# Layer 1 attention: when the value products of heads 0 to 3 are issued

## The chip, the cores and the metric

The kernel runs on one core of a Trainium2 chip, as one launch. The metric is the device time of that core in microseconds (us). A core has five engines that each run their own instruction stream in order: TensorE (PE, with its weight loads shown apart as PEld), VectorE (DVE), ScalarE (ACT), GpSimd (POOL) and SyncE (SP), which in this kernel issues most of the DMAs. Engines wait for each other by semaphores. Matrix products land in PSUM[...].

## The reference

Two residual attention blocks over x of 8 samples, 512 channels, 32x32 pixels (1024 tokens), all in float32, 8 heads of 64 channels. Layer 0 is ordinary attention. Layer 1, which the change concerns, mixes the heads' scores before the softmax and normalises the weights of each head over the whole map after it:

```
x = x + layer0(groupnorm(x))
x = x + layer1(groupnorm(x))

# layer1, per sample
q, k, v = w_q @ xf, w_k @ xf, w_v @ xf          # (8 heads, 64, 1024)
attn = einsum('bhdq,bhdT->bhqT', q, k) * scale  # scores
attn = einsum('gh,bhqT->bgqT', w_head, attn)    # mixed over heads
attn = softmax(attn, axis=-1)
attn = (attn - mean) / sqrt(var + EPS)          # mean, var of each head's whole map
attn = attn * in_gamma + in_beta
out  = einsum('bhqT,bhdT->bhqd', attn, v)       # value products
out  = out @ w_proj.T + b_proj
```

## The kernel before

Layer 0 takes the first 1813 us; then layer 1 goes through the 8 samples one after the other. All matrix products are float32. A sample has 4 blocks of 256 queries (QB) and 4 blocks of 256 keys (KB), and the work is cut into half steps, `half_step(x, ag)` (L1879), with x from 0 to 36. Each half step does parts of three stages, at three places in the same pipeline:

- Scores of half step x, `scores(x, i)` (L1645), for i = 0 and 1: 8 products of 64x64 weights with 256 columns into one PSUM tile. The tile is copied to the buffer `raw`, by VectorE (L1671) for i = 0 in odd half steps and by ScalarE (L1673) otherwise. Through DMAs of 256 KB, `regroup` (L1675, issue L1682), `raw` is rearranged to `re`, heads onto partitions. There are 32 half steps with scores.
- The mix over heads of half step y = x - 4 (MLAG, L1283), `mix(y, j)` (L1695), for j = 0 and 1: 32 products of 64x64 weights with 64 columns (L1706) into one PSUM tile, then an exponential on ScalarE (L1712) from there into `e`. The epool has two such tiles (L1269).
- For half step w = x - 5: the sums of e and e squared (`squares` on ScalarE, L1723; `sum_e` and `sum_e2` on VectorE, L1730 and L1734), and the value products `values(w, 0)` for heads 0 to 3 and `values(w, 1)` for heads 4 to 7 (L1740): 4 products each of 128x64 weights with 256 columns (L1752), which accumulate over 8 half steps in two PSUM tiles `acc[0]` and `acc[1]`, one buffer each (L1274).

In float32 each product shows as two matmuls and two weight loads in the profile, so a group of scores is 16 matmuls, a mix 64, a group of values 8. Scores and mixes share a rotation of three PSUM tiles (`ps_m`, L1275): a group may start when the group three tiles earlier has been copied out. Value products have tiles of their own.

The order on every engine is the order in which the code calls things. On TensorE a half step is scores 0, mix 0, values 0, scores 1, mix 1, values 1. After the last mix or values instruction a regroup DMA is triggered, one for each call, and after scores a `piece` (L1687): a part of the next sample's input or weights. Eight regroup DMAs make one `re` tile, over two half steps.

Every 8th half step (`first`, L1881: x = 13, 21 and 29) the accumulators of the query block just finished have to be copied out by `leave` (L1762; heads 0 to 3 by ScalarE, L1774, heads 4 to 7 by VectorE, L1772) before new value products may start in them. At the end of the half step before it stands `totals` (L1776), the column sums. Half steps 0 to 3 have scores alone, half step 4 scores and mix, and from x = 32 (NX) on there are no more scores: the last five half steps are mix and value products, with projection products of the next sample between them, put there by an agenda (`ag`), which also runs normalisations, reciprocals and divisions at given half steps.

Of the kernel before, what the change touches and what calls it, by code (L numbers as in the profile page):

```python
# [467 lines left out]
def tile_two_attention_layers(  # L468
# [796 lines left out]
    with ExitStack() as l1:  # L1265
# [14 lines left out]
        NX = 2 * NQB * NKB  # L1280
# [181 lines left out]
        def k_leave():  # L1462
            for fn in due:
                fn()
            due.clear()
# [173 lines left out]
        class Attention1:  # L1639
# [239 lines left out]
            def half_step(self, x, ag):  # L1879
                y, w = x - MLAG, x - MLAG - 1  # L1880
                first = 0 < w < NX and w % QLAG == 0  # L1881
                if first:

                    self.scores(x, 0)
                    self.leave(w // QLAG - 1)
                if 0 <= w < NX:
                    self.squares(w, 0)
                    self.sum_e(w, 0)
                if x < NX and not first:
                    self.scores(x, 0)  # L1890
                if 0 <= w < NX:
                    self.squares(w, 1)
                    self.sum_e(w, 1)
                k_leave()
                if 0 <= w < NX:
                    self.sum_e2(w, 0)
                    self.sum_e2(w, 1)
                if 0 <= y < NX:
                    self.mix(y, 0)
                if 0 <= w < NX:  # L1900
                    self.values(w, 0)
                if x < NX:
                    self.scores(x, 1)
                if 0 <= y < NX:
                    self.mix(y, 1)
                ag.run(x - 0.75)
                if x <= MLAG or x >= NX:
                    self.regroup(n=NR)
                if x >= NX:
                    self.piece(n=len(self.pieces))  # L1910
                ag.run(x - 0.5)
                if 0 <= w < NX:
                    self.values(w, 1)
                    self.e.pop(w)
                    if w % QLAG == QLAG - 1:
                        qb = w // QLAG
                        self.totals(qb)
                        if qb < NQB - 1:
                            ag.at(x + 2, lambda: self.reciprocals(qb, ag, x + 2))
                            ag.at(x + 6, lambda: self.divide(qb))  # L1920
                ag.run(x)
# [139 lines left out]
```

## Time and profile before

| what | us |
|---|---|
| median of 3 runs (4268.31 to 4270.03) | 4268.98 |
| the profiled execution | 4269.45 |
| its span in the profile | 4267.5 |
| first scores of layer 1, sample 0, start at | 1813.3 |
| layer 1, from one sample's first scores to the next's | 309 to 323 |
| mean granted TensorE clock, share of full speed | 0.997 |

Section 5 of the page gives the groups of instructions with their busy time, the mean length of one and the idle time ahead of them. Those of layer 1's half steps:

```profile
L1706 PE MATMUL m<-wmix,re 64*64 64x64 f32 x32768 | 591.0, 219 | 22.4 <-issue 19.7
L1712 ACT ACTIVATE e<-m 128x1024 f32<-128x1024 f32 x512 | 528.1, 1032 | 147.1 <-PE m L1706 142.6
L1752 PE MATMUL a<-e,v 128*64 128x256 f32 x4096 | 556.3, 392 | 25.0 <-ACT q L1774 20.9
L1656 PE MATMUL s<-k,q 64*64 64x256 f32 x8192 | 555.8, 389 | 5.8 <-DVE q L1512 2.6
L1673 ACT COPY raw<-s 128x1024 f32<-128x1024 f32 x368 | 373.4, 1015 | 251.9 <-PE s L1656 229.6
L1671 DVE COPY raw<-s 128x1024 f32<-128x1024 f32 x144 | 176.0, 1223 | 102.5 <-PE s L1656 93.8
```

To read a line: the source line, the engine, the operation, what it writes and reads, the tile of the array (64*64 is 64 rows by 64 columns of it[...]), the shape, the count; then busy us and the mean in ns; then the engine's idle time just ahead and what ended most of it. "issue" means that the trace shows nothing that the engine waited for. The mean of a matmul is longer than its share of the busy time, because several run at once.

In the timeline, a line is a merged run of like instructions of one engine: start and length in us, engine, line, operation, what it writes and reads, count, and idle time ahead in brackets.

### The profile page before, as it was taken

The page shows a single profiled execution, that of the slowest core. Times are in us where ns is not written, and L with a number is a line of the kernel's source. Part 1 is how long each engine was busy: PE and PEld are TensorE (multiplying, and loading weights), DVE is VectorE, ACT ScalarE, POOL GpSimd, SP SyncE. Part 2 cuts the span into 40 slices and gives each one's busy share as a digit, 9 for nine tenths or more (in the row PEclk, how much of TensorE's full clock was granted, in tenths as well). Part 3 has the DMA queues.
Part 4 walks back from the last instruction along what each step waited for, and adds up shares of the span by engine and source line. Part 5 has one row for each costly group of instructions (what it writes and reads, how often), then busy time and mean ns, then how long its engine had stood idle before and what let it go on. Part 6 is the DMA issues. An engine that isn't in the chain of part 4 may idle for free.

```text
span 4267.5 us, 131379 instructions
## 1 busy us (share of the span) xinstructions
PE 4158.3 (97%) x58572; PEld 2213.3 (52%) x58572; DVE 2862.8 (67%) x3780; ACT 2319.2 (54%) x2735; POOL 53.3 (1%) x86
## 2 busy tenths in 40 slices
PE   7999999999999999999999999999999999999998
PEld 4353535353535353466466466466466466465565
DVE  4748484848484848558668668578578578587587
ACT  1717171727272726268268278187187286286385
POOL 0000000000000000000000000000000000000000
PEclk9999999999999999999999999999999999999999
DMA  4213131212121212167377287277386385485474
GB/s 148 78 49 109 47 110 45 86 45 85 45 85 45 84 47 83 56 169 192 111 180 190 93 199 186 99 197 185 96 202 166 103 205 155 121 204 142 136 179 136
DMA packets 253872, 521.99 MB, mean 122 GB/s; under 512 B 51889, under 2 KB 59441, under 8 KB 246641
## 3 DMA queue, kind: packets, MB, share of 16 engines
q1 hardware_dynamic: 248416, 510.71, 42.4%
q8 instruction: 461, 7.55, 0.7%
q0 software_dynamic: 2576, 0.69, 0.3%
q10 hardware_dynamic: 2304, 2.10, 0.2%
q14 instruction: 115, 0.93, 0.1%
HBM read 197.16 MB, written 46.92 MB: 57 GB/s over the span
## 4 chain that ended last, share of the span: by engine, by line
PE 90%; DVE 4%; ACT 2%; DMA 2%; issue 1%; SPq 0%; POOL 0%; DVEq 0%; ACTq 0%; POOLq 0%
PE a L1752 11%; PE s L1656 11%; PE m L1706 11%; PE s L1083 10%; PE a L1109 10%; PE pp_p L903 5%; PE pk_p L903 5%; PE pq_p L903 4%; PE pv_p L903 4%; PE pk L1400 4%; PE pq L1400 4%; PE pv L1475 4%; PE pp L1400 3%; PE t L1783 2%; ACT q L1774 1%
## 5 line engine op out<-in xcount | busy, mean ns | idle before, releaser
L1706 PEld LDWEIGHTS m<-wmix,re 64*64 64x64 f32 x32768 | 580.8, 135 | 117.1 <-issue 57.5
L1088 ACT ACTIVATE e<-s 128x1024 f32<-128x1024 f32 x512 | 497.2, 1026 | 234.2 <-PE s L1083 233.8
L1706 PE MATMUL m<-wmix,re 64*64 64x64 f32 x32768 | 591.0, 219 | 22.4 <-issue 19.7
L1712 ACT ACTIVATE e<-m 128x1024 f32<-128x1024 f32 x512 | 528.1, 1032 | 147.1 <-PE m L1706 142.6
L1752 PE MATMUL a<-e,v 128*64 128x256 f32 x4096 | 556.3, 392 | 25.0 <-ACT q L1774 20.9
L1730 DVE TENSOR_TENSOR z<-z,e 128x1024 f32<-128x1024 f32 x448 | 537.8, 1218 | 62.3 <-ACT e L1712 62.3
L1734 DVE TENSOR_TENSOR z<-z,e 128x1024 f32<-128x1024 f32 x448 | 534.2, 1219 | 44.4 <-ACT e L1723 43.7
L1656 PE MATMUL s<-k,q 64*64 64x256 f32 x8192 | 555.8, 389 | 5.8 <-DVE q L1512 2.6
L1096 DVE TENSOR_TENSOR zacc<-zacc,e 128x1024 f32<-128x1024 f32 x384 | 468.6, 1220 | 90.4 <-ACT e L1088 69.3
L1673 ACT COPY raw<-s 128x1024 f32<-128x1024 f32 x368 | 373.4, 1015 | 251.9 <-PE s L1656 229.6
L1083 PE MATMUL s<-q,k 64*64 64x512 f32 x4096 | 490.1, 593 | 2.3 <-ACT e L1088 2.3
L1109 PE MATMUL a<-e,v 64*64 64x512 f32 x4096 | 484.1, 589 | 0.0
L1723 ACT ACTIVATE e<-e 128x1024 f32<-128x1024 f32 x448 | 461.7, 1062 | 0.0
L1656 PEld LDWEIGHTS s<-k,q 64*64 64x64 f32 x8192 | 267.7, 132 | 272.9 <-issue 169.4
L1752 PEld LDWEIGHTS a<-e,v 128*64 128x64 f32 x4096 | 250.8, 136 | 147.1 <-ACT q L1774 24.2
L1109 PEld LDWEIGHTS a<-e,v 64*64 64x64 f32 x4096 | 156.7, 133 | 282.8 <-issue 282.8
L1083 PEld LDWEIGHTS s<-q,k 64*64 64x64 f32 x4096 | 147.9, 133 | 275.2 <-issue 241.4
L1671 DVE COPY raw<-s 128x1024 f32<-128x1024 f32 x144 | 176.0, 1223 | 102.5 <-PE s L1656 93.8
L1475 PE MATMUL pv<-re,y 128*128 128x512 f32 x480 | 214.5, 600 | 0.0
L1475 PEld LDWEIGHTS pv<-re,y 128*128 128x128 f32 x480 | 89.1, 191 | 113.3 <-issue 112.6
L903 PE MATMUL pv_p<-left_v,tmp 128*128 128x256 f32 x512 | 115.0, 383 | 4.2 <-DVE tmp L932 4.2
L1480 DVE COPY v<-pv 128x512 f32<-128x512 f32 x30 | 20.7, 689 | 139.6 <-ACT v L1479 139.6
(315 smaller groups left out, 4050.3 us busy)
## 6 DMA issues: line engine op xcount, KB each, us to landing
re<-raw SPq DMA_DIRECT2D x1024, 256.0 KB
rzb<-zd SPq DMA_DIRECT2D x256, 128.0 KB
left_q<-left_q SPq DMA_DIRECT2D x17, 1792.0 KB
left_p<-left_p SPq DMA_DIRECT2D x17, 1792.0 KB
left_k<-left_k SPq DMA_DIRECT2D x10, 1792.0 KB
x<-in_x_dram SPq DMA_DIRECT2D x32, 512.0 KB
x<-x SPq DMA_DIRECT2D x64, 256.0 KB
left_v<-left_v SPq DMA_DIRECT2D x8, 1792.0 KB
```

The source lines that it names most:

```text
L903: nc.tensor.matmul(out, st, mv, start=start, stop=(k == 1), skip_group_check=True)
L1083: nc.tensor.matmul(ps[c * D : c * D + D, m], k[r, hp, k0 : k0 + D], q[r, hp, ts(f, FB)], start=True, stop=True,)
L1088: nc.scalar.activation(e[i], ps, AF.Exp, scale=S0 * S0)
L1109: nc.tensor.matmul(acc[g][a][m * D : m * D + D], v[rows, kc, ts(2 * hp + m, D)], e[i][rows, m], start=(kc == 0), stop=(kc == NG - 1),)
L1400: nc.tensor.matmul(self.ps[m][:, i], w[:, left, k * HC + i * P : k * HC + i * P + P], right[:, k], start=(k == 0 and m != 2), stop=(k == 1 ...
L1475: nc.tensor.matmul(ps[:, m], y_t[b][:, c, ts(2 * i + m, P)], w[:, c], start=(c == 0), stop=(c == NCC - 1),)
L1656: last = nc.tensor.matmul(pv[c * D : c * D + D, m, j], qo_t[b][r, 2 * qb + j, hp, ts(c, D)], k_t[b][r, hp, ts(kb, KB)], start=True, stop=True,
L1706: last = nc.tensor.matmul(ps[c * D : c * D + D, a, ts(r, D)], self.re[t, r][rows, j, k0 : k0 + D], wmix[rows].rearrange("p g i -> p (g i)" ...
L1712: nc.scalar.activation(self.e[y][:, j], ps.rearrange("p a c -> p (a c)"), AF.Exp)
L1730: nc.vector.tensor_add(self.z[:, j], self.z[:, j], self.e[y][:, j])
L1734: nc.vector.tensor_add(self.z2[:, j], self.z2[:, j], self.e2[j])
L1752: last = nc.tensor.matmul(self.acc[w][two * D : two * D + D, s].rearrange("p (c i) -> p c i", i=Q8), v_t[b][:, kc, ts(g, D)], e[:, g], sta ...
```

## The change

The call of `values(w, 0)` is moved from behind the first mix of the half step to its end, ahead of `values(w, 1)`, and behind the agenda's slots x - 0.75 and x - 0.5.

```diff
@@ half_step @@
                 if 0 <= y < NX:
                     self.mix(y, 0)
-                if 0 <= w < NX:
-                    self.values(w, 0)
                 if x < NX:
                     self.scores(x, 1)
                 if 0 <= y < NX:
                     self.mix(y, 1)
                 ag.run(x - 0.75)
...
                 ag.run(x - 0.5)
                 if 0 <= w < NX:
+                    self.values(w, 0)
                     self.values(w, 1)
                     self.e.pop(w)
```

On TensorE a half step becomes scores 0, mix 0, scores 1, mix 1, values 0, values 1. The regroup DMA that `values(w, 0)` triggers moves with it on SP's queue: it now follows the one of the second mix. No instruction is added or taken away, and no buffer changes.

## The prediction

> **What bounds the kernel now.** I read the page first, then the busy time of two full half steps, then TensorE's timeline through an ordinary half step, through the odd places and through a stall. The page:
>
> ```profile
> PE 4158.3 (97%) x58572; PEld 2213.3 (52%) x58572; DVE 2862.8 (67%) x3780; ACT 2319.2 (54%) x2735; POOL 53.3 (1%) x86
> q8 instruction: 461, 7.55, 0.7%
> PE 90%; DVE 4%; ACT 2%; DMA 2%; issue 1%; SPq 0%; POOL 0%; DVEq 0%; ACTq 0%; POOLq 0%
> ```
>
> TensorE is busy 97% of the span and is 90% of the chain of waits. Remember the second line: 58572 matmuls and 58572 weight loads come in 461 instruction blocks of 16 KB. The view by windows (two half steps; PE, PEld, DVE, ACT, POOL, clock, DMA share, GB/s) and the timeline of one half step (start, length):
>
> ```profile
> 2485.00:2497.00 12.00, 12.00 (x364) 8.55 (x359) 10.42 (x10) 10.78 (x12) 0.00 (x0) 1.00 0.86 222
> ```
>
> ```profile
> 2307.85 1.09 PE L1656 MATMUL s<-k,q 64*64 64x256 f32 x16
> 2308.77 1.11 PE L1706 MATMUL m<-wmix,re 64*64 64x64 f32 x64
> 2309.81 1.08 PE L1752 MATMUL a<-e,v 128*64 128x256 f32 x8
> 2310.82 1.09 PE L1656 MATMUL s<-k,q 64*64 64x256 f32 x16
> ```
>
> TensorE never rests, ScalarE and VectorE are at 87 to 90%. From start to start, scores to mix take 0.91 us, mix to value products 1.04, value products to scores 1.01: 2.97 us, twice per half step, 5.94. [...] Two places show other neighbours:
>
> ```profile
> 2783.54 1.11 PE L1706 MATMUL m<-wmix,re 64*64 64x64 f32 x64
> 2784.47 1.05 PE L1656 MATMUL s<-k,q 64*64 64x256 f32 x16
> 2785.34 0.97 PE L1706 MATMUL m<-wmix,re 64*64 64x64 f32 x51
> 2787.65 0.45 PE L1706 MATMUL m<-wmix,re 64*64 64x64 f32 x13 [1.34 <-issue]
> ...
> 2379.48 1.95 PE L1752 MATMUL a<-e,v 128*64 128x256 f32 x16
> ```
>
> Mix to scores is 0.93, the scores to mix after it 0.87, and two groups of value products end to end take 1.95, so the second costs 1.95 - 1.08 = 0.87. The fourth line shows something else: TensorE stands for 1.34 us in the middle of a group, released by nothing the trace shows ("issue"). Counting matmuls and their loads from 2783.54, 128 + 32 + about 96 = 256 instructions have been issued: one 16 KB block. The DMA view, cut into narrow windows, puts one instruction packet at 2785.22, lasting 0.96 us. TensorE goes on 1.47 us after its end. [...] Two stalls a block apart in an ordinary half step say the same, 4.02 us:
>
> ```profile
> 3720.21 1.09 PE L1706 MATMUL m<-wmix,re 64*64 64x64 f32 x58 [0.47 <-issue]
> 3721.22 1.08 PE L1752 MATMUL a<-e,v 128*64 128x256 f32 x8
> 3722.24 1.09 PE L1656 MATMUL s<-k,q 64*64 64x256 f32 x16
> 3723.15 0.87 PE L1706 MATMUL m<-wmix,re 64*64 64x64 f32 x46
> 3724.23 0.50 PE L1706 MATMUL m<-wmix,re 64*64 64x64 f32 x18 [0.20 <-issue]
> ```
>
> Last, the steps marked `first` in the code, where the accumulators must be copied out:
>
> ```profile
> 2321.51 1.08 PE L1752 MATMUL a<-e,v 128*64 128x256 f32 x8 [0.87 <-ACT q L1774]
> ...
> 2327.27 1.01 ACT L1673 COPY raw<-s 128x1024 f32<-128x1024 f32 x1
> ```
>
> The first value products stand 0.94 us longer than 1.04 (24 times, 22.6 us). Over all mix-to-value steps of layer 1 the timeline has 64.8 us above 1.04 each; the other 42 us are almost all block stalls.
>
> [...] 64x64 to 128x64 and back costs 1.04 and 1.01, staying in a mode 0.87 to 0.93. [...]
>
> **The change, part by part.** It adds and removes nothing; each half step's order on TensorE goes from s m a s m a to s m s m a a.
>
> *Transitions.* After: 0.91 + 0.93 + 0.87 + 1.04 + 0.87 + 1.01 = 5.63 or 5.64 us against 5.94: 0.30 less. Per sample, half steps 5 to 31 have all three parts, 27; six belong to the `first` pairs below. The other 21 x 8 x 0.30 = 50.4 us. In half steps 32 to 35 (mix and values, then projection work) m a m a becomes m m a a; no row shows m after m, but same-mode steps are 0.87 to 0.93, so about 0.3 again: 4 x 7 x 0.3 = 8.4. Two mixes in a row use up a block in 1.9 us, which costs stalls (below), so I take 5.4; the bounds are 0 and 8.4. The last sample has no projection there and VectorE sums take four times 1.14, 4.6 us, a step: nothing.
>
> *Score tiles.* Scores and mixes rotate through three PSUM tiles, so the second mix needs the first scores copied out. It comes 2.71 us after the first scores start, formerly 3.97. Copy on VectorE (odd half steps): 1.09 + 0.07 + 1.22 = 2.38; on ScalarE 2.17. Both fit, by 0.26 and 0.5 us with the semaphore's 0.07, if the engine is free. ScalarE's six operations in an even half step start 0.92 apart, 5.5 us; VectorE's nine in two half steps 1.14 apart, 10.3 of 11.3 us. Both keep up. Behind the waiting mix stand only the value products. One sample's normalisation plus division before half step 27 makes VectorE late by about 0.44, with crumbs elsewhere: 3.5 us in all.
>
> *`first` steps.* Value products now come after the second mix, 3.75 us in, and ScalarE has left the accumulators at 2.85: the 0.94 goes. But ScalarE is back to back from there: its next first-score copy (2327.27 above) ends 9.67 us after the step's start whatever TensorE does, and the second mix needs it at 5.63 + 2.71 = 8.34. It waits 1.40. The pair takes 9.74 + 1.04 + 0.87 + 1.01 = 12.66 against 12.91: 24 x 0.25 = 6.0 us.
>
> *Instruction blocks.* Weight loads and matmuls are 32, 128 and 16 per s, m and a: 352 a half step, 11 blocks in 8. Formerly the shortest block, from a mix's start, was 1.04 + 1.01 + 0.91 + 0.66 = 3.62 us; now m s m have no values between them and it is 0.93 + 0.87 + 0.78 = 2.58. Of the eleven positions, those under 4.0 us were 3.62 three times and about 3.7; now 2.59, 2.99 and 3.18, others 4.27 up. With 4.0 us a block, 8 half steps lost 3 x 0.38 + 0.3 = 1.44, 27 such sets 39 us, which the 42 confirm; now 1.41 + 1.01 + 0.82 = 3.24, 88 us. So 49 us more. Where ScalarE's 1.40 falls with a stall they overlap, some 0.4 us in each of 24 pairs: 10 back.
>
> *DMA and SP.* Regroup DMAs are triggered by the ends of mixes and values, one each, so three now follow each other (1.0 us apart), then two pieces and one regroup. All eight per tile still precede the next tile's scores, the last one behind a mix instead of values, so their landing has 4.5 us instead of 3.8 until its use. SP's order follows TensorE's; nothing is queued longer. Cost nothing, except that the DMA share, 0.86 there, rises by a twentieth, which can lengthen the block fetch.
>
> Sum: 50.4 + 5.4 + 6.0 - 3.5 = 58.3 us without the blocks, - 49 + 10 = 19.3 with them. The profiled execution took 4269.45 (span 4267.5 and 1.95 around it), so 4250; the median of the runs, 4268.98, is 0.5 less, within the rounding.
>
> **Rivals.** *The fetch does not grow.* [...] the 2.58 us blocks then cost no more than now: 4269.45 - 58 = 4211. Against it: the first half step with mixes (s m s m) shows that stall in seven of eight samples. *The score-tile wait takes the gain.* If VectorE or ScalarE starts the first copy 0.3 us later than laid out, on top of the margins, each half step gives back its 0.30, the blocks then get their old time, and some 4267 is left, no change. For it: both engines are near 90%; against it: stalls give them time. *Slower, by the block fetch.* Place: the second mix of a half step. If three regroups in a row and the denser DMA lengthen a block from 4.0 to 4.3 us, the stalls become 118, 79 more than now: 4269.45 - 58 - 10 + 79 = 4280; at 4.5 us 152, so 4314. It decides from 4.2 us on. For it: with the DMA engines 80 to 95% busy the packet starts 1.5 us after the block before it is begun (median), with under 30%, 0.8 us.
>
> **How the numbers follow.** Forecast 4250 (own range 4228 to 4261) 0.5; fetch unchanged 0.12; score tiles 0.17; slower 0.21. The range 4210 to 4284 leaves out the far ends of the first and last. A change within 0.2%, 8.5 us, is not told from none: faster 0.59 (most of the forecast and the second case), same 0.20, slower 0.21.
>
> **What would show it.** Right: value products as groups of 16 matmuls of 1.95 us; ordinary half steps without a stall at 5.63; no wait for the accumulator copies; the second mix of the half step after a `first` one waiting for ScalarE's copy of scores; "issue" idle time in mixes about doubled, by 0.8 to 1.4 us each. Wrong: half steps all alike above 5.7 with a wait for a score copy, which would mean that the tiles bind; or "issue" time unchanged.

## The result, and the profile after

The changed kernel takes 4306.05 us (median of 4 runs, 4303.42 to 4309.25), the kernel before beside it 4269.5: the ratio is 1.0084, 95% interval 1.0071 to 1.0097. It is 0.84% slower, where I had forecast a gain of 0.45%. It is one of the rivals that came true: the wait for instruction blocks.

From the page of the changed kernel, the busy times and the groups that were shown of before (busy, mean ns | idle before, and what ended it):

```profile
PE 4115.0 (96%) x58572; PEld 2222.7 (52%) x58572; DVE 2862.6 (67%) x3780; ACT 2303.1 (54%) x2735; POOL 53.4 (1%) x86
...
q8 instruction: 461, 7.55, 0.7%
...
PE 84%; ACT 5%; DVE 4%; issue 4%; DMA 3%; SPq 0%; ACTq 0%; DVEq 0%
```

```profile
L1706 PE MATMUL m<-wmix,re 64*64 64x64 f32 x32768 | 599.7, 220 | 102.2 <-issue 82.2
...
L1656 PE MATMUL s<-k,q 64*64 64x256 f32 x8192 | 551.0, 384 | 14.3 <-ACT e L1712 5.8
L1752 PE MATMUL a<-e,v 128*64 128x256 f32 x4096 | 512.9, 390 | 14.8 <-issue 14.5
```

TensorE does the same instructions in 43 us less busy time (4115.0 against 4158.3; the value products alone 512.9 against 556.3), and the span is 36 us longer. The idle time ahead of mixes went from 22.4 to 102.2 us, 82.2 of it "issue". In the chain, TensorE fell from 90% to 84% and issue rose from 1% to 4%.

The timeline of TensorE in the changed kernel, a half step without a stall and the start of the next:

```profile
2503.81 1.09 PE L1656 MATMUL s<-k,q 64*64 64x256 f32 x16
2504.73 1.11 PE L1706 MATMUL m<-wmix,re 64*64 64x64 f32 x64
2505.66 1.05 PE L1656 MATMUL s<-k,q 64*64 64x256 f32 x16
2506.52 1.11 PE L1706 MATMUL m<-wmix,re 64*64 64x64 f32 x64
2507.57 1.95 PE L1752 MATMUL a<-e,v 128*64 128x256 f32 x16
2509.44 1.09 PE L1656 MATMUL s<-k,q 64*64 64x256 f32 x16
```

The steps are close to those forecast: scores to mix 0.92, mix to scores 0.93, scores to mix 0.86, the value products in one group of 1.95. The half step takes 5.63 us. But in many others TensorE stands in the middle of a group, for nothing that the trace shows. From one of these places to the next in a sample it is a multiple of 128 matmuls, that is of 256 instructions with the weight loads, to within one or two matmuls. The page has 461 packets of 16 KB on the instruction queue for 2 x 58572 matmuls and loads, 254 to a packet. So I read these places as the ends of instruction blocks.

Such a stall, with what SP issued ahead of it:

```profile
2891.19 1.11 PE L1706 MATMUL m<-wmix,re 64*64 64x64 f32 x64
2892.12 1.05 PE L1656 MATMUL s<-k,q 64*64 64x256 f32 x16
2892.99 0.87 PE L1706 MATMUL m<-wmix,re 64*64 64x64 f32 x47
2896.16 0.50 PE L1706 MATMUL m<-wmix,re 64*64 64x64 f32 x17 [2.30 <-issue]
2896.59 3.61 PE L1752 MATMUL a<-e,v 128*64 128x256 f32 x16
```

```profile
2888.53 2.39 SPq L1682 DMA_DIRECT2D re<-raw  x3
2891.43 0.48 SPq L1321 DMA_DIRECT2D left_k<-left_k  x1
2892.36 0.53 SPq L1682 DMA_DIRECT2D re<-raw  x1
2893.22 0.48 SPq L1321 DMA_DIRECT2D left_k<-left_k  x1
```

And the DMA view of the 5 us from 2891 to 2896 (queue, packets, MB, share of the 16 engines):

```profile
q1 hardware_dynamic: 638, 1.12, 97.6%
q8 instruction: 1, 0.02, 1.6%
```

The block began near 2891.2, the start of the first mix. Just before, three regroups of 256 KB had been issued in 2.4 us, and the DMA engines are 99% busy in the view (97.6 and 1.6). Narrow windows put the one instruction packet at 2893.42, lasting 1.24 us, and TensorE goes on 1.50 us after its end. So this block took 5.0 us, where the prediction had reckoned 4.0.

The same reading over all half steps 5 to 31: from the start of a block to the start of the next block's packet, plus the packet's length, plus the 1.48 us that passed in the median from its end to the next instruction where TensorE stood. Call this the fetch time. For the blocks that begin within 0.4 us of the start of a first mix its median is 3.61 us before (52 blocks) and 4.09 after (55 blocks), the upper quartile 4.01 and 4.82. Idle time at block ends ("block stalls"), over all of layer 1, is 36 us before and 120 us after (every stretch over 0.36 us, less 0.1 of ordinary spacing).

The last line of the stall shows one thing more: the value products take 3.61 us instead of 1.95. The view by windows (PE, PEld, DVE, ACT, POOL, granted clock, DMA share, GB/s) has the granted clock at 0.50 there:

```profile
2897.00:2900.00 3.00, 3.00 (x16) 1.43 (x12) 2.54 (x3) 1.66 (x2) 0.00 (x0) 0.50 0.47 110
```

Half steps 5 to 30 of the changed kernel have five such stretches of 3.4 us, each behind a stall of 1.9 to 2.3 us; together they cost 7.7 us. The kernel before has none there. Six other stalls in these half steps, of 1.95 to 2.42 us, and one of 2.62 us ending at 2983.68 have none behind them; what decides isn't settled. The mean granted clock was 0.993 to 0.996 in the four runs of the changed kernel, 0.997 in the kernel before.

Where the 36 us come from, by the starts of the groups:

| part of the trace | before | after | difference |
|---|---|---|---|
| half steps 5 to 30, 8 samples, at the pace without stalls | 1302.4 | 1248.0 | -54.4 |
| the same, time above that pace | 39.0 | 136.9 | +97.9 |
| from half step 31 to the end of a sample's value products | 383.1 | 373.8 | -9.3 |
| the rest of the span | | | +2.1 |

Of the 97.9 us in the second row, block stalls in these half steps are 79 (27.5 before, 106.5 after); 19 are other losses, the 7.7 us at half clock among them.

### The profile page after: what moved, and what is told of

The parts are those of the page before. It is cut to its first block, busy times and chain, and to the rows that moved or that the text cites. A ratio compares the mean times of both kernels' runs of the same rounds, so it can differ in the third digit from the quotient of the medians.

```text
span 4303.8 us, 131247 instructions
## 1 busy us (share of the span) xinstructions
PE 4115.0 (96%) x58572; PEld 2222.7 (52%) x58572; DVE 2862.6 (67%) x3780; ACT 2303.1 (54%) x2735; POOL 53.4 (1%) x86
## 4 chain that ended last, share of the span: by engine, by line
PE 84%; ACT 5%; DVE 4%; issue 4%; DMA 3%; SPq 0%; ACTq 0%; DVEq 0%
PE s L1083 10%; PE m L1706 10%; PE a L1109 10%; PE a L1752 10%; PE s L1656 8%; PE pp_p L903 5%; PE pk_p L903 4%; PE pq_p L903 4%; PE pv_p L903 4%; PE pk L1400 4%; PE pq L1400 4%; PE pv L1475 4%; PE pp L1400 3%; PE t L1783 2%; DMA re<-raw 2%
## 5 line engine op out<-in xcount | busy, mean ns | idle before, releaser
L1706 PE MATMUL m<-wmix,re 64*64 64x64 f32 x32768 | 599.7, 220 | 102.2 <-issue 82.2
L1752 PE MATMUL a<-e,v 128*64 128x256 f32 x4096 | 512.9, 390 | 14.8 <-issue 14.5
L1752 PEld LDWEIGHTS a<-e,v 128*64 128x64 f32 x4096 | 276.6, 138 | 166.3 <-issue 43.3
```

What stands on the lines that cost most here:

```text
L1706: last = nc.tensor.matmul(ps[c * D : c * D + D, a, ts(r, D)], self.re[t, r][rows, j, k0 : k0 + D], wmix[rows].rearrange("p g i -> p (g i)" ...
L1752: last = nc.tensor.matmul(self.acc[w][two * D : two * D + D, s].rearrange("p (c i) -> p c i", i=Q8), v_t[b][:, kc, ts(g, D)], e[:, g], sta ...
```

## The experiments

Theory F: the loss is the wait for instruction blocks, which are used up faster in the new order and also arrive later, since three regroup DMAs in a row crowd the DMA engines. Theory G: the arrival is no later by the crowding. Theory S: the time is lost in waits for the PSUM tiles of scores. All times are beside the kernel before on the same chip, which took about 4277 us there; so ratios are compared. The code excerpts leave lines out.

**Regroups in pairs, last one later.** The new order on TensorE stays; the second mix's trigger goes to the second scores.

```diff
 # scores(x, i)
                 if x > MLAG:
                     self.piece(last)
+                if x > MLAG and i == 1:
+                    self.regroup(last)
 # mix(y, j)
-                self.regroup(last)
+                if j == 0 or y + MLAG >= NX:
+                    self.regroup(last)
```

> The changed order on TensorE (s m s m a a), but the regroup DMA that the second mix of a half step triggers is triggered by the second scores instead, so that regroups come in pairs (gaps of about 1, 2, 1, 2 us) as in the kernel before, not three in a row. Theory F (an instruction block takes 4.5 instead of 4.0 us because three regroups in a row crowd the DMA engines): block stalls fall from about 137 us in half steps 5 to 31 to near 88, time about 4257. Theory G (the round trip stays as long as in the changed kernel whatever the bunching; only the amount of DMA traffic and the short blocks count): 4300 to 4310. Theory S (score-tile waits cost the time): no change, 4300 to 4310.

Measured: 4286.05, ratio 1.0024 (1.0017 to 1.0031). Over two thirds of the loss are gone, more than G or S allow, but not all that F expected. The waits of its TensorE (total, times, longest) say what came in their place:

```profile
PE m L1708 <- issue: 52.1, 57, 2.1
PE m L1708 <- DMA re<-raw: 23.1, 34, 1.8
PE m L1708 <- ACT raw L1675: 12.1, 19, 0.7
```

Block stalls are 80 us, and the fetch time of blocks beginning at a first mix is 3.72 us in the median, near the 3.61 before the change. But the last regroup of a tile now stood behind the second scores, nearer to its use, and mixes wait for regrouped scores, which cost 1.7 us in the changed kernel.

**Regroups in pairs, last one as in the changed kernel.** The trigger of the second value products goes to the first scores of the next half step.

```diff
 # scores(x, i)
+                if x > MLAG and i == 0:
+                    self.regroup(last)
 # values(y, w)
-                self.regroup(last)
+                if w == 0:
+                    self.regroup(last)
```

> The changed order (s m s m a a); the regroup DMA that the second group of value products triggers is triggered by the first scores of the next half step instead. So regroups come in pairs as in the kernel before, and the last of each tile is still behind a mix, 4.5 us ahead of its use, while the run with spread regroups had it 3.6 us ahead and waited for it. Theory F (three regroups in a row lengthen the block fetch): stalls for blocks near 80 us as in the spread run, without its waits for regrouped scores: about 4255 to 4265 beside 4269 of the kernel before. Theory G (crowding does not matter; the spread run only moved time about): 4290 to 4310.

Measured: 4280.23, ratio 1.0004 (0.9996 to 1.0011). One DMA trigger of four, moved by one group, takes back 0.8 of 0.84%. Its waits:

```profile
PE m L1708 <- issue: 60.5, 71, 2.1
PE m L1708 <- ACT raw L1675: 15.8, 23, 0.7
PE m L1708 <- DMA re<-raw: 7.5, 12, 1.8
```

Block stalls are 91 us by the count used above, near the 88 of the prediction; the fetch time of blocks that begin at a first mix is 3.59 us. G falls. The expected 4255 to 4265 (beside 4269) is missed all the same: with pairs the new order is no faster than the old, only as fast.

**Three in a row in the old order.** The converse: s m a s m a with the first mix's trigger at the first scores.

```diff
 # scores(x, i)
+                if x > MLAG and i == 0:
+                    self.regroup(last)
 # mix(y, j)
-                self.regroup(last)
+                if j == 1:
+                    self.regroup(last)
```

> The order of the kernel before (s m a s m a), but the regroup DMA that the first mix triggers is triggered by the first scores of the half step instead, so that three regroups follow each other 1 us apart as in the changed kernel. Theory F: the block takes about 4.5 us here too, and the stalls rise from 39 towards 110 us: 4310 to 4340. Theory G: the traffic is the same, so about 4269, at most 4280. Theory S: 4269.

Measured: 4279.61, ratio 1.0009 (1.0000 to 1.0018). F's numbers are wrong here: some 4 us, not 40 to 70; by the time alone G fits as well. Block stalls rise from 36 to 41 us. In half steps 5 to 19 the run is not quite the converse that was meant: the first scores trigger a piece of 128 KB ahead of the regroup, so that SP's queue has one between the second regroup and the third.

```profile
2497.57 1.52 SPq L1684 DMA_DIRECT2D re<-raw  x2
2499.61 0.31 SPq L1356 DMA_DIRECT2D y<-x  x1
2499.97 0.53 SPq L1684 DMA_DIRECT2D re<-raw  x1
```

The closest three regroups of a half step are issued within 2.44 us there (median, first to third), not within 1.86 as in the changed kernel, and the fetch time at a first mix is 3.85 us, against 3.73 before and 4.34 in the changed kernel. In half steps 20 to 30 few pieces are left, and this is the closer comparison (22 to 24 blocks in each median):

| half steps 20 to 30 | three regroups within, us | fetch time at a first mix, us | block stalls, us |
|---|---|---|---|
| kernel before | 2.86 | 3.51 | 8 |
| this run | 2.06 | 3.99 | 10 |
| changed kernel | 1.86 | 4.05 | 38 |
| pairs, last one later | 2.77 | 3.71 | 26 |
| pairs, last one as in the changed kernel | 2.73 | 3.45 | 26 |

Here the fetch gets nearly as long as in the changed kernel, against G, and the old order still loses only 2 us more. So here crowding cost little where the shortest block lasts 3.62 us (10 us of block stalls against 8), and more together with the short blocks of the new order (38 us against 26 with pairs).

**A quarter of the regroup traffic, both orders.**

```diff
 # regroup, from the third key block of each sample on
-    dma = nc.sync.dma_start(out=self.re[t, r], in_=self.raw[t][r::NR])
+    rows = P // NR if t < 2 else P // NR // 4
+    dma = nc.sync.dma_start(
+        out=self.re[t, r][: rows * H], in_=self.raw[t][r::NR][:rows]
+    )
```

> The changed kernel with a quarter of each regroup DMA (from the third key block of each sample on, 4 of the 16 rows are moved, the rest of the regrouped scores stays as it was), so the mix reads partly old scores. Theories F and G (the time is lost waiting for instruction blocks): with the DMA engines mostly idle a block takes about 0.8 + 0.95 + 1.47 = 3.2 us, only the blocks of 2.6 and 3.0 us still stall, some 20 us: 4306 - 137 + 20, about 4190, and some 40 us faster than the light version of the kernel before. Theory S: the waits for score copies stay, so it is not faster than the light version of the kernel before.

> The kernel before with a quarter of each regroup DMA (as in the light version of the changed kernel). Theories F and G: no block under 3.6 us is left to stall, 4269 - 39 = 4230. Theory S says nothing of it beyond 4230 to 4269.

Both kernels leave out three quarters of each of these regroups and serve for their times alone. Measured: 4194.1 in the new order, ratio to the full kernel before 0.9806 (0.9790 to 0.9822), and 4234.0 in the old order, 0.9899 (0.9883 to 0.9916). TensorE's waits in layer 1, first the new order, then the old:

```profile
PE m L1709 <- ACT raw L1673: 17.8, 24, 0.7
PE m L1709 <- issue: 15.5, 27, 1.3
```

```profile
PE a L1755 <- ACT q L1777: 20.9, 24, 0.9
PE m L1709 <- issue: 5.1, 5, 1.4
```

This settles between F and S. With the DMA engines 29% busy (0.86 in the full kernel before, in the same 12 us), the change makes the kernel 40 us faster, as expected: 58 of the sum without blocks, less some 20 for blocks too short even then. The waits for score copies are all still there in the new order (17.8 us, 16.4 in the changed kernel) and aren't what costs. The light runs also take part of the traffic away from every other transfer, so not all of their gain is the block fetch. In half steps 5 to 30 the time above the pace falls by 107 us in the new order, 87 of them block stalls, and by 32 in the old, 19 of them block stalls; the issue time in mixes falls from 82.2 to 15.5 and from 19.7 to 5.1.

**An order with space around each mix.** Scores, scores, mix, values, values, mix: the same single change of tile (64*64 to 128*64) and back, but at least 3.2 us to a block, as I estimated from the steps of the trace. The excerpt is shown against the changed kernel.

```diff
 # half_step
+                if x < NX:
+                    self.scores(x, 1)
                 ...
                 if 0 <= y < NX:
                     self.mix(y, 0)
-                if x < NX:
-                    self.scores(x, 1)
+                if 0 <= w < NX:
+                    self.values(w, 0)
+                    self.values(w, 1)
                 if 0 <= y < NX:
                     self.mix(y, 1)
```

> Another order of the half step: both scores, first mix, all value products, second mix (s s m a a m). It has one change of tiling mode and back, like the changed kernel, but 1.9 us of other work on either side of each mix, so that the shortest instruction block is 3.2 us instead of 2.6. Regroups: first scores, second scores, first mix, second mix in odd half steps; first scores, first mix, first values, second mix in even ones, the last of a tile behind a first mix. Theory F: half steps of 5.62 us, and with 4.0 to 4.2 us a block stalls of 30 to 65 us (216 half steps): 4230 to 4260, below the kernel before. If the time of the changed kernel came from waits for PSUM tiles or accumulators (theory S), this one, with more distance between a group and the reuse of its tile, would also fall to 4230 or lower, but then with its block stalls unchanged at 120 us or more it would not: 4290.

Measured: 4300.66, ratio 1.0056 (1.0042 to 1.0070): neither what F expected nor what S did. Block stalls are 65 us, as F has them, but TensorE waited for other things:

```profile
PE m L1709 <- issue: 35.3, 52, 1.8
PE m L1709 <- DMA re<-raw: 24.8, 36, 2.1
PE pk L1400 <- ACT sum L1409: 7.7, 7, 1.1
PE t L1787 <- DVE z L1737: 7.6, 12, 0.9
```

Regrouped scores came late, a projection waited for a copy that value products used to cover, and the half steps with totals took 9.1 us in the mean against 8.4 in the changed kernel, since VectorE's last sum, behind ScalarE's squares, came late. Mending these three gave the last run.

> The even order (s s m a a m) mended where its first run lost time outside the block fetch: the second squares stand ahead of the second scores' copy on ScalarE, so that VectorE's last sum is done before the totals; in odd half steps regroups behind first scores, second scores, first mix and second mix, in even ones behind first scores, first mix and both value groups; in the last half steps the value products stay behind the projection products. Theory F: blocks still stall some 65 us, but the 30 us of waits for regrouped scores, the 1.6 us in each of 24 half steps with totals and 8 us in the last half steps go: about 4235 to 4250, below the kernel before. If the even order has some other cost that I have not seen: 4270 to 4300.

Its edits: `squares(w, 1)` ahead of the second `scores`; value products behind the projection from half step 32 on; regroup triggers as told.

```profile
PE m L1709 <- issue: 47.2, 57, 1.9
PE m L1709 <- DMA re<-raw: 9.7, 17, 1.5
PE a L1756 <- issue: 8.3, 10, 2.5
PE t L1788 <- DVE z L1738: 5.6, 8, 1.0
```

Measured: 4268.96 beside 4277.14, ratio 0.9978 (0.9970 to 0.9986). That is faster than the kernel before by 0.22% and than the changed one by about 1%, less than the 4235 to 4250 I had expected: its block stalls are 77 us, not some 65. The profiled run, from which these are read, took 4260.67, 8 us less than the median.

## Why the prediction was wrong

*Transitions*: right. 5.63 us a half step and 1.95 us for the joined value products were measured as forecast. In half steps 5 to 30 the paced time fell by 54.4 us, where 20 x 8 x 0.30 = 48.0 and the 6.0 of the `first` pairs make 54.0.

*`first` steps*: right in the sum, not in the parts. Forecast 12.66 us for the pair; the trace has 5.98 + 6.64 = 12.62. The 12.91 I had read for the pair before held a small block stall; most pairs took 6.88 + 5.94 = 12.82, so the gain is 4.8 us, not 6.0. The wait moved from the accumulators to ScalarE, as told, but not as one wait of 1.40 for the copy of scores: 0.3 us of it comes earlier, as a wait for an exponential to leave the score tiles. In the changed kernel's waits:

```profile
PE m L1706 <- ACT raw L1673: 16.4, 23, 0.7
...
PE s L1656 <- ACT e L1712: 5.8, 21, 0.3
```

*Half steps 32 to 35*: too low, about 9 us where I took 5.4 and put the bound at 8.4. Where the rest comes from isn't settled.

*Score tiles*: right in the ordinary half step, where no such wait shows: 5.63 us is the most frequent time, and lies at the pace without waits. (The 3.97 us that I gave for the distance before the change is a slip: 0.91 + 1.04 + 1.01 + 0.91 is 3.87. Nothing rests on it.)

*Instruction blocks*: here the sum failed. That the shorter blocks would stall more was right, the term was mis-sized. I took 4.0 us a block for both orders (the stalls shown in the prediction have 4.11, from 2783.54 to 2787.65, and 4.02), which gave 88 us of stalls against 39, and subtracted 10 for overlap: 39 us more. Measured are 120 against 36: 84 more. The pairs experiment divides the error. With the old kernel's pairs the stalls are 91 us, so the arithmetic on block lengths was nearly right and its figure of 4.0 us served for that spacing. The remaining 29 us belong to three regroups in a row. One reading behind it was too simple: that a block is there a fixed time after the block ahead starts (last section).

*DMA and SP*: this is the step behind it that failed. I saw that three regroups would follow each other, checked that they land in time, and wrote "Cost nothing, except that the DMA share, 0.86 there, rises by a twentieth, which can lengthen the block fetch"; the longer fetch went into a rival instead of the forecast. The reason was off as well: over half steps 5 to 30 the DMA share is 0.77 before and 0.75 after. The traffic did not grow; three regroups came closer together, and they end just where the short block begins. The rival "slower, by the block fetch" had 118 us of stalls and 4280 us at 4.3 us a block. The stalls, 120, came out like that, but the time was 4306: the rest of its sum, which it shared with the forecast, was too good by some 20 us. I gave it 0.21.

*The overlap of 10 us*: not seen. Other losses above the stall-free pace rose instead, by about 19 us (97.9 - 79), of which the prediction had 3.5; 7.7 are the stretches at half clock, and what makes up the rest isn't settled.

The sum: 19.3 us less was forecast, the profiled span is 36.3 longer, an error of 55.6. Block stalls in half steps 5 to 30 make 30 of it (79 against 49), the overlap 10, other losses 15 to 16, the rest of the span 2; the first and third rows of the table together fell 2 more than forecast (63.7 against 61.8).

What stays open too: why with pairs the new order only draws level. It has 64 us less of paced work (54.4 + 9.3). In half steps 5 to 30 it has 51 us more of block stalls (78 against 27.5) and 20 more of other losses (32 against 11.5), 7.5 of them in all waits for regrouped scores. That closes the sum to some us, but the other losses are not traced one by one, and the two traces are from chips on which the kernel before differs by 7.5 us.

## What to carry to other kernels

In a kernel of many short matmuls, count the instructions on TensorE's queue as well as their time. Here the shortest block of 256 lasts 2.58 us by the sum of its steps, formerly 3.62, the fetch time at a first mix was 4.09 us in the median, formerly 3.61, and TensorE stood for 120 us at block ends, formerly 36, for nothing that the trace shows. When a step is moved, its DMAs move with it. That they land in time was not enough here: waits for regrouped scores were 1.7 us in the changed kernel, and one trigger moved by one group still took back 0.8%. Ask what else they now share the DMA engines with. In the two orders with other groups between the mixes block stalls were 36 us (old order) and 65 to 77 (space around each mix), against 80 to 120 with scores alone between two mixes; what such an order loses elsewhere has to be counted too.

## What the runs showed of the hardware

The packet of an instruction block started, in half steps 5 to 31, in the median 1.29 us after the block ahead of it had begun in the kernel before and 1.43 after the change, at the earliest 0.9 us ahead of that. When a block is asked for, no trace shows. The fetch time went with what else was on the DMA engines: for blocks that begin at a first mix, 2.8 us in the median with a quarter of the regroups, 3.6 to 3.7 with regroups in pairs, 4.1 with three in a row in the new order and 3.9 with three nearly in a row in the old. Of the 0.5 us between the kernel before and the changed one there, the packet itself lengthened by 0.2 (median 0.98 to 1.20), and the wait for its start by 0.3 (1.14 to 1.47). I had not expected that moving one DMA trigger by a single group of matmuls, with no change in bytes or in the order on TensorE, would be worth 0.8% of the time. Nor that the granted clock could fall to 0.50 for 3.4 us behind an idle stretch of TensorE of 1.9 to 2.3 us, as it did five times in half steps 5 to 30 of the changed kernel, and not behind six others of 1.95 to 2.42 us there.
